# One core, attention over kept tokens: the first pair's products in four PSUM banks, other buffers and slots for the first two batches

## The chip, the cores and the metric

The kernel runs on one core of a Trainium2 chip. The metric is device time in microseconds. The engines that compute are TensorE (PE, with PEld for its weight loads), VectorE (DVE), ScalarE (ACT) and GpSimd (POOL); SyncE (SP) issues DMAs. Each has its own instruction stream and runs it in order; they wait for each other by semaphores.

## What is computed

Eight batches of attention with eight heads, with queries, keys and values from one projection, a 0/1 mask over tokens, and a residual. From the reference:

```python
B, D, T = x.shape                 # 8, 512, 1024
dk = D // NH                      # 8 heads of 64
xt = jnp.transpose(x, (0, 2, 1))
q = xt @ Wq.T
qh = q.reshape(B, T, NH, dk).transpose(0, 2, 1, 3)
scores = scale * jnp.einsum('bhqd,bhkd->bhqk', qh, qh)
logits = (scores * cmask + (1.0 - cmask) * NEG) * rmask
attn = jax.nn.softmax(logits, axis=-1)
ctx = jnp.einsum('bhqk,bhkd->bhqd', attn, qh)
out = ctx.transpose(0, 2, 1, 3).reshape(B, T, D) @ Wo.T
return x + jnp.transpose(out, (0, 2, 1))
```

A masked token (mask 0) as a key gets weight 0; as a query it attends evenly to all tokens, so that its output is the mean of all values.

## The kernel before

About half of the 1,024 tokens of a batch are kept by the mask. The kernel gathers the kept tokens, at most 543 (`NK` = `SHORT` = 544 places, the last one for the mean of all tokens), and runs attention on them alone. Inputs with more kept tokens go to two other versions, which don't run here.

**Pairs and slots.** The work is 32 pairs: 8 batches of 4 pairs of heads (`pairs`, numbered p; `pr` is the pair in its batch). A pair has five slots, k = 0 to 4, one for each chunk of 128 keys, in `order`: first the short chunk `LAST` (with tokens 512 to 575 of the ring), then the four full ones. In each slot `late` issues `scores` of that chunk (TensorE, line 785 or 807; exponentials by ScalarE, line 793 or 810), and then what the tables give to slot (pr, k): `TURN`, `SEARCH`, `GATHER`, `LOAD`, `FEATURES` and others. For the second batch the tables with `_LATER` hold, and `LATER` for its search. Last come the tasks of `slots_of`, among them `attend_half` (line 831), `project` (703) and `collect` (659). The order on each engine is the order in the program: `manual_schedule` moves nothing.

**A batch's way in.** `load_piece` loads x in eight pieces of 256 KB, two halves of the tokens (tag `x`, two buffers). `turn` transposes a quarter of the tokens on VectorE (581) into a buffer `xt` (two of them), whose four stores to DRAM (`xd`) SP issues at the end of the slot (589). `search` finds on VectorE (634, 637), for each place, which token it holds, from the ranks that `load_ranks` has broadcast. `gather` fetches the rows of the kept tokens from `xd` by an indirect DMA on POOL (646), five of them, the fifth with 32 rows; `keep_step` ahead of it makes POOL wait for an exponential of that slot. `collect` turns the rows back on TensorE (659) and a copy puts them into `xcs`; `project` multiplies them by Wq. For the second batch the collects are in slots (2,3) and (2,4). `add_features` sums x over tokens on ScalarE (600), `mean_of` makes the mean on VectorE (605, 607).

**The ring.** `rings[0]` holds the projection of the first pair: 544 columns, and from column `NK` on the last 32 columns (`END`) three times over.

**The first batch and `early`.** The first pair of the first batch takes another way, so as not to wait for a gather. `early` counts the kept tokens, makes ranks and `chosen` (0/1 matrices that select tokens, `choose`, 444), and calls `project_first`. There TensorE turns a part of Wq (482), `search_first` broadcasts the ranks by sixteen matmuls (451) and ScalarE counts by `Sign` with a sum (464), five times; `project_all` multiplies blocks of 128 tokens, all of them, by that part of Wq (493), from block 7 down to 0, into `tall`, one PSUM tile of two banks. `copy_two` (503) copies two blocks to `q`, `square` (510) squares four for `lengths` (513). `order_columns` (1171) reorders Wq on ScalarE. On VectorE come two `turn_first` (423), `choose`, `sources_of_first` (475, which needs the signs), the other two `turn_first`, pads and penalties (534 to 537), and the lengths up to `first_top` (546). The products `short` (555) select the kept tokens' columns from `q`; among them stands the transpose of `first_top` (764) that gives the first bias (766 to 769). `add_first` (435) sums x on VectorE. ScalarE copies `short` to the ring (568).

Then `late` begins, behind a branch that each engine takes by itself when it gets there. VectorE copies the ring's end columns there (1322), POOL issues the first batch's gathers (646), the load of the second batch's ranks (622) and of Wo (1162), and SP loads the second batch's x (385), whose buffers come free when `add_first` has read the first batch's.

Of the kernel before, what the change touches and what calls it, by code (L numbers as in the profile page):

```python
# [10 lines left out]
F32 = mybir.dt.float32  # L11
# [10 lines left out]
Q = 32  # L22
# [284 lines left out]
def attention_of_kept_tokens(ctx, tc, x, mask, wq, wo, out, ident, wqT, woT, verdict, flag):  # L307


    nc = tc.nc  # L310
# [107 lines left out]
    def turn_first(i):  # L418

        n = T // NQ  # L420
        r, at = divmod(i * n, NB)
        xt = sb.tile([P, n // Q, P], F32, tag="xt", name=f"xt_0_{i}", bufs=2)
        nc.vector.transpose(
            xt.rearrange("p k (d f) -> p k d f", d=ND),
            xs[0][r][:, :, at : at + n].rearrange("p d (k t) -> p k d t", t=Q),
        )
        for a in range(A):
            to = xds[0][i * n : (i + 1) * n, a * P : (a + 1) * P]
            queue = nc.gpsimd if a % 2 else nc.sync
            queue.dma_start(to.rearrange("(k t) c -> t k c", t=Q), xt[a * Q : (a + 1) * Q, :, :])  # L430

    def add_first(r):
        if r == NN - 1:
            xbars[0] = keep.tile([P, ND, NN], F32, name="xbar_0")
        nc.vector.tensor_reduce(xbars[0][:, :, r], xs[0][r], axis=AX.X, op=ALU.add)
# [41 lines left out]
    def project_first(chosen, mcol):  # L477

        wT = sb.tile([P, ND, P], F32, tag="junka", name="wqT_0", bufs=1)
        pw = bank("wq_0_t")  # L480
        for d in range(ND):
            nc.tensor.transpose(pw[:, d * P : (d + 1) * P], woT[:, 0, d::ND], ident)
        nc.scalar.copy(wT.rearrange("p d e -> p (d e)"), pw)
        search_first(seen["rank"])
        tall = ps.tile([P, 2, NB], F32, tag="s", name="tall")
        q = [sb.tile([P, G, P], F32, tag="oc", name=f"q_0_{r}", bufs=NC) for r in range(NN)]
        sq = sb.tile([P, T], F32, tag="junk", name="sq_0", bufs=1)
        H = LONG // 2

        def project_all(i):  # L490
            r, at = divmod(i * P, NB)
            for d in range(ND):
                nc.tensor.matmul(
                    tall[:, r, at : at + P],
                    xs[0][r][:, d, at : at + P],
                    wT[:, d, :],
                    start=(d == 0),
                    stop=(d == ND - 1),
                )

        def copy_two(i):
            r, at = divmod(i * P, NB)
            nc.scalar.copy(
                q[r][:, i % G : i % G + 2, :].rearrange("p c e -> p (c e)"),
                tall[:, r, at : at + 2 * P],
            )

        def square(r):
            at = slice(r * NB, (r + 1) * NB)
            nc.scalar.activation(sq[:, at], tall[:, r, :], AF.Square)  # L510

        def lengths(r):
            nc.vector.tensor_reduce(
                first_len[:, r * G : (r + 1) * G, :].rearrange("p c h -> p (c h)"),
                sq[:, r * NB : (r + 1) * NB].rearrange("p (c d) -> p c d", d=DK),
                axis=AX.X,
                op=ALU.add,
            )

        for i in reversed(range(NT)):  # L520
            project_all(i)
            if i % 2 == 0:
                copy_two(i)
            if i % G == 0:
                square(i // G)
        order_columns()
        turn_first(2)
        turn_first(3)
        for i in (3, 2, 1, 0):
            choose(i, chosen[i])  # L530
# [6 lines left out]
        nc.vector.tensor_scalar(pens, pads, NEG, None, ALU.mult)  # L537
        lengths(1)
        lengths(0)
        nc.vector.tensor_tensor(  # L540
            first_len,
            first_len,
            mcol[:, :NT].unsqueeze(2).to_broadcast([P, NT, 2]),
            ALU.mult,
        )
        nc.vector.tensor_reduce(
            first_top, first_len.rearrange("p c h -> p (c h)"), axis=AX.X, op=ALU.max
        )
        short = ps.tile([P, 2, NB], F32, tag="s", name="short")
        for i in reversed(range(NT)):  # L550
            w = chosen[i].shape[1]
            for hf in range(2):
                n = min(w - hf * H, H)
                if n > 0:
                    nc.tensor.matmul(
                        short[:, hf, :n],
                        q[i // G][:, i % G, :],
                        chosen[i][:, hf * H : hf * H + n],
                        start=(i == NT - 1),
                        stop=(i * P <= hf * H),  # L560
                    )
            if i == G:
                tops[pairs[0]] = first_top
                bias_of(pairs[0], first_bias)
        add_first(1)
        add_first(0)
        mean_of(0)
        nc.scalar.copy(
            rings[0][:, :LONG].rearrange("p (h n) -> p h n", h=2), short[:, :, :H]
        )  # L570

    def turn(b, i):
# [609 lines left out]
            )  # L1182
        (copy or nc.scalar.copy)(wT[:, d, :], pt)

    def early():
        BC = B * NT
        mrow = keep.tile([BC, P], F32, name="mrow")
        nc.sync.dma_start(mrow, mask.rearrange("b (c p) -> (b c) p", p=P))
# [118 lines left out]
        nc.vector.tensor_copy(origin, placed)  # L1307

    def late(n):
        fit_to(n)  # L1310
        nc.vector.tensor_scalar(lacks, kept, float(-NK), None, ALU.add)
        queries_of(0)
        load_batch(1)
# [2 lines left out]
        for i in range(NC):  # L1316
            gather(0, i)
        load_ranks(1, nc.gpsimd)
        weights["wo"] = load_weights(wo, "wo", nc.gpsimd)
        qT = qTs[pairs[0]] = rings[0]  # L1320
        biases[pairs[0]] = first_bias
        nc.vector.tensor_copy(
            qT[:, NK:W].rearrange("p (r k) -> p r k", k=END),
            qT[:, NK - END : NK].unsqueeze(1).to_broadcast([P, (W - NK) // END, END]),
        )
# [176 lines left out]
def kernel(  # L1502
# [22 lines left out]
    def kept_tokens(n):  # L1525

        with ExitStack() as pools:
# [1 line left out]
                pools, tc, x, mask, wq, wo, out, ident, wqT, woT, verdict, flag  # L1529
            )  # L1530
            with tc.manual_schedule():
                early()
# [41 lines left out]
```

## Time and profile before

| | us |
|---|---|
| Median of three runs | 702.32 (700.89 to 702.73) |
| The profiled execution | 700.78 |
| Its span, first to last instruction | 699.0 |
| PE busy in the span | 657.0 (94%) |
| PEld busy | 400.1 (57%) |
| DVE busy | 366.5 (52%) |
| ACT busy | 395.0 (57%) |
| POOL busy | 181.6 (26%) |
| mean granted TensorE clock | 0.968 |

Busy is the time in which an engine had an instruction under way. The chain of waits starts at the last instruction and goes back, at each step, to what released it; its shares say where time was spent that something else would have had to take. In the timeline a line gives start and length in us, engine, source line and operation, output and inputs by the program's names, how many instructions were merged, and in brackets the idle time before the first and what ended it. A window gives, for a stretch of the span, each engine's busy time, and the clock that TensorE was granted as a share of full speed.

### The profile page before, as it was taken

The page shows a single profiled execution, that of the slowest core. Times are in us where ns is not written, and L with a number is a line of the kernel's source. Part 1 is how long each engine was busy: PE and PEld are TensorE (multiplying, and loading weights), DVE is VectorE, ACT ScalarE, POOL GpSimd, SP SyncE. Part 2 cuts the span into 40 slices and gives each one's busy share as a digit, 9 for nine tenths or more (in the row PEclk, how much of TensorE's full clock was granted, in tenths as well). Part 3 has the DMA queues.
Part 4 walks back from the last instruction along what each step waited for, and adds up shares of the span by engine and source line. Part 5 has one row for each costly group of instructions (what it writes and reads, how often), then busy time and mean ns, then how long its engine had stood idle before and what let it go on. Part 6 is the DMA issues. An engine that isn't in the chain of part 4 may idle for free.

```text
span 699.0 us, 12228 instructions
## 1 busy us (share of the span) xinstructions
PE 657.0 (94%) x4212; PEld 400.1 (57%) x4212; DVE 366.5 (52%) x1061; ACT 395.0 (57%) x1055; POOL 181.6 (26%) x304
## 2 busy tenths in 40 slices
PE   8799979999999999999999999999999999999953
PEld 7666546656565655556565655556565655554422
DVE  5555864435556554756446653837455433724462
ACT  4347747855576556746585656755574655444400
POOL 4700310040034402440044302450143202332240
PEclk7999989999999999999999999999999999999975
DMA  7552560442856577765786477864974575348558
GB/s 244 161 206 81 162 182 2 119 160 88 185 157 214 163 176 164 216 211 138 181 216 230 157 174 167 257 225 110 205 185 126 124 159 125 107 115 215 121 185 242
DMA packets 99169, 116.31 MB, mean 166 GB/s; under 512 B 10471, under 2 KB 76519, under 8 KB 99102
## 3 DMA queue, kind: packets, MB, share of 16 engines
q1 hardware_dynamic: 82894, 77.23, 42.9%
q0 software_dynamic: 11984, 36.16, 16.3%
q10 hardware_dynamic: 4224, 2.10, 1.0%
q8 instruction: 34, 0.56, 0.3%
q14 instruction: 33, 0.27, 0.1%
HBM read 72.78 MB, written 42.67 MB: 165 GB/s over the span
## 4 chain that ended last, share of the span: by engine, by line
PE 77%; DMA 9%; DVE 4%; issue 2%; ACT 1%; SPq 1%; POOL 0%; POOLq 0%; DVEq 0%; ACTq 0%
PE s L785 19%; PE av L831 17%; PE po L952 14%; PE pq L703 14%; DMA g<-od,block_origin 3%; PE xc L659 3%; PE s L807 3%; PE v L728 2%; PE pa L980 2%; DMA xr<-in_x_dram 1%; PE top L764 1%; DVE xr L1029 1%; DMA xin<-xd,source 1%; DMA xd<-xt 1%; DMA g<-od,origin 1%
## 5 line engine op out<-in xcount | busy, mean ns | idle before, releaser
L793 ACT ACTIVATE e<-s,bias 128x544 f32<-128x544 f32 x248 | 174.7, 709 | 68.0 <-PE s L785 65.8
L785 PE MATMUL s<-qT 64*128 64x272 f32 x1024 | 168.4, 418 | 1.0 <-issue 0.7
L785 PEld LDWEIGHTS s<-qT 64*128 64x128 f32 x1024 | 97.5, 187 | 67.8 <-issue 29.7
L831 PE MATMUL av<-e,v 128*64 128x272 f32 x1024 | 133.1, 403 | 0.0
L703 PE MATMUL pq<-xc,wqT 128*128 128x272 f32 x496 | 119.3, 393 | 0.0
L952 PE MATMUL po<-woT,cT 128*128 128x512 f32 (+1 forms) x448 | 107.5, 434 | 0.0
L703 PEld LDWEIGHTS pq<-xc,wqT 128*128 128x128 f32 x496 | 93.1, 193 | 17.8 <-issue 0.8
L831 PEld LDWEIGHTS av<-e,v 128*64 128x64 f32 x1024 | 68.5, 138 | 56.7 <-issue 24.4
L964 POOL DMA_DIRECT2D od<-oc x56 | 30.2, 551 | 254.9 <-ACT oc L962 254.7
L952 PEld LDWEIGHTS po<-woT,cT 128*128 128x128 f32 (+1 forms) x448 | 46.8, 150 | 47.0 <-issue 46.2
L1066 POOL DMA_INDIRECT g<-od,block_origin x56 | 56.4, 1007 | 50.2 <-DVE o L1026 12.4
L1026 DVE STREAM_TRANSPOSE o<-g 128x512 f32<-128x512 f32 x56 | 39.3, 702 | 35.9 <-DMA g<-od,block_origin 34.4
L822 DVE CUSTOM_DVE_ANT_0 junk<-el,part 128x272 f32<-128x272 f32 x64 | 28.1, 438 | 54.9 <-ACT el L810 43.8
L810 ACT ACTIVATE el<-s,bias 128x544 f32<-128x544 f32 x31 | 22.1, 714 | 57.5 <-PE s L807 56.4
L1062 POOL COPY step<-e 1x1 f32<-1x1 f32 x77 | 16.7, 217 | 142.0 <-ACT e L793 141.6
L711 ACT COPY qT<-pq 128x272 f32<-128x272 f32 (+1 forms) x62 | 23.6, 381 | 51.7 <-PE pq L703 49.1
L751 DVE TENSOR_REDUCE len<-sq 128x10 f32<-128x640 f32 x31 | 25.3, 817 | 47.4 <-ACT sq L749 47.4
L793 ACT ACTIVATION_READ_ACCUMULATOR e<-s,bias 128x1 f32 x248 | 48.6, 196 | 0.0
L1029 DVE TENSOR_TENSOR xr<-o,xr 128x512 f32<-128x512 f32 x56 | 38.8, 693 | 14.5 <-DMA xr<-in_x_dram 8.0
L646 POOL DMA_INDIRECT xin<-xd,source x40 | 39.7, 993 | 16.8 <-issue 8.8
L766 DVE TENSOR_REDUCE m<-top 128x1 f32<-128x128 f32 x32 | 9.2, 289 | 57.8 <-PE top L764 55.8
L581 DVE STREAM_TRANSPOSE xt<-x 128x1024 f32<-128x1024 f32 x28 | 34.8, 1242 | 3.2 <-DMA xd<-xt 3.1
(183 smaller groups left out, 718.3 us busy)
## 6 DMA issues: line engine op xcount, KB each, us to landing
x<-in_x_dram SPq DMA_DIRECT2D x64, 256.0 KB
xd<-xt SPq DMA_DIRECT2D x120, 128.0 KB
xr<-in_x_dram SPq DMA_DIRECT2D x28, 512.0 KB
out_dram<-xr SPq DMA_DIRECT2D x24, 512.0 KB
rb<-row SPq DMA_DIRECT2D x60, 160.0 KB
od<-oc POOLq DMA_DIRECT2D x28, 256.0 KB
rank<-ranks SPq DMA_DIRECT2D x6, 512.0 KB
out_dram<-xr SPq DMA_DIRECT2D x8, 256.0 KB
```

Source lines behind the costliest of these rows:

```text
L581: nc.vector.transpose(xt.rearrange("p k (d f) -> p k d f", d=ND), xs[b][r][:, :, at : at + n].rearrange("p d (k t) -> p k d t", t=Q),)
L646: nc.gpsimd.indirect_dma_start(out=xin[:n, :], out_offset=None, in_=xds[b], in_offset=bass.IndirectOffsetOnAxis(ap=searches[b][2][:n, i : ...
L703: nc.tensor.matmul(pq[:, :KH], wqT[:, d, pr * P : (pr + 1) * P], xcs[b][:, d, cols], start=(d == 0), stop=(d == ND - 1),)
L785: nc.tensor.matmul(ss[h][:, hf, :KH], qT[heads[h], keys], qT[heads[h], queries[hf]], start=True, stop=True,)
L793: nc.scalar.activation(e[:, :, h, :], ss[h][:, :, :KH], AF.Exp, bias=bias, scale=SCALE, accum_out=sums[pair[1] % 2][:, h, c : c + 1],)
L822: nc.vector.tensor_tensor_reduce(junk[:, :KH], e[:, 0, h, :], parts[b], 1.0, 0.0, ALU.mult, ALU.add, ends[pr % 2][:, h : h + 1])
L831: nc.tensor.matmul(av[head, :KH], v[keys, c, head], e[keys, hf if c < LAST else 0, h, :], start=(c == first), stop=(c == last),)
L952: nc.tensor.matmul(po[k * n : (k + 1) * n, :w], cTs[b, pr][:, i * P : i * P + n], woT[:, pr, k * w : (k + 1) * w], start=(pr == 0), stop=( ...
L964: nc.gpsimd.dma_start(ods[b][places[i], k * w : (k + 1) * w], oc[k * n : (k + 1) * n, :w])
L1026: nc.vector.transpose(o.rearrange("p k t -> p (k t)"), gs[b, i])
L1029: nc.vector.tensor_tensor(to, o, to, ALU.add)
L1066: nc.gpsimd.indirect_dma_start(out=g, out_offset=None, in_=ods[b], in_offset=bass.IndirectOffsetOnAxis(ap=block_origin[:, b, i : i + 1], a ...
```

## The change

The first batch's products go to four PSUM banks of one tile each, two blocks to a bank. `search_first` moves from ahead of all products to behind the first four blocks (7 to 4), their copies and `square(1)`, with eight transposes of the identity (`warm(8)`) in its old place. The squares read `q` in SBUF; `square(0)` comes after the last copy. `turn_first` takes its buffers from the tag `e` (six buffers, used later by the exponentials), so four quarters have one each; for that `fit_to` is called in `early`. `add_first` and `mean_of` go ahead of the lengths. The transpose of `first_top` goes from behind block 4 to behind block 2 of `short`. The ring's end columns are copied from `short` by ScalarE. In the tables, the second batch's turns, searches and gathers move.

```diff
@@ turn_first
-        xt = sb.tile([P, n // Q, P], F32, tag="xt", name=f"xt_0_{i}", bufs=2)
+        xt = sb.tile([P, 2, 2, KH], F32, tag="e", name=f"xt_0_{i}", bufs=6)
+        xt = xt.rearrange("p a b k -> p (a b k)")[:, : n // Q * P].rearrange("p (k c) -> p k c", c=P)
@@ project_first
-        search_first(seen["rank"])
-        tall = ps.tile([P, 2, NB], F32, tag="s", name="tall")
+        warm(8)
+        tall = [bank(f"tall_{i}") for i in range(NT // 2)]
...
-        sq = sb.tile([P, T], F32, tag="junk", name="sq_0", bufs=1)
+        sq = {}
...
-                    tall[:, r, at : at + P],
+                    tall[i // 2][:, i % 2 * P : (i % 2 + 1) * P],
...
-                q[r][:, i % G : i % G + 2, :].rearrange("p c e -> p (c e)"),
-                tall[:, r, at : at + 2 * P],
+                q[i // G][:, i % G : i % G + 2, :].rearrange("p c e -> p (c e)"),
+                tall[i // 2][:, : 2 * P],
...
         def square(r):
-            at = slice(r * NB, (r + 1) * NB)
-            nc.scalar.activation(sq[:, at], tall[:, r, :], AF.Square)
+            t = sb.tile([P, NC, P], F32, tag="sq", name="sq_0_1", bufs=1) if r else sb.tile(
+                [P, NT, P], F32, tag="junk", name="sq_0_0", bufs=1
+            )
+            sq[r] = t[:, :G, :].rearrange("p c e -> p (c e)")
+            nc.scalar.activation(sq[r], q[r].rearrange("p c e -> p (c e)"), AF.Square)
...
             project_all(i)
             if i % 2 == 0:
                 copy_two(i)
-            if i % G == 0:
-                square(i // G)
+            if i == G:
+                square(1)
+                search_first(seen["rank"])
+        square(0)
         order_columns()
...
         nc.vector.tensor_scalar(pens, pads, NEG, None, ALU.mult)
+        add_first(1)
+        add_first(0)
+        mean_of(0)
         lengths(1)
         lengths(0)
...
-            if i == G:
+            if i == 2:
                 tops[pairs[0]] = first_top
                 bias_of(pairs[0], first_bias)
-        add_first(1)
-        add_first(0)
-        mean_of(0)
         nc.scalar.copy(
             rings[0][:, :LONG].rearrange("p (h n) -> p h n", h=2), short[:, :, :H]
         )
+        nc.scalar.copy(
+            rings[0][:, NK:W].rearrange("p (r k) -> p r k", k=END),
+            short[:, 1, NK - END - H : NK - H].unsqueeze(1).to_broadcast([P, (W - NK) // END, END]),
+        )
@@ early, late
-    def early():
+    def early(n):
+        fit_to(n)
...
-        fit_to(n)
...
-        qT = qTs[pairs[0]] = rings[0]
+        qTs[pairs[0]] = rings[0]
         biases[pairs[0]] = first_bias
-        nc.vector.tensor_copy(
-            qT[:, NK:W].rearrange("p (r k) -> p r k", k=END),
-            qT[:, NK - END : NK].unsqueeze(1).to_broadcast([P, (W - NK) // END, END]),
-        )
...
-        TURN_LATER = [(0, 4), (1, 0), (1, 1), (1, 2)]
+        TURN_LATER = [(0, 3), (0, 4), (1, 0), (1, 1)]
...
-        LATER = {(1, 1): (0,), (1, 2): (1,), (1, 3): (2, 3), (1, 4): (4,)}
+        LATER = {(0, 4): (0,), (1, 0): (1,), (1, 1): (2,), (1, 2): (3,), (1, 3): (4,)}
...
-        GATHER_LATER = {(1, 4): (0,), (2, 0): (1,), (2, 1): (2,), (2, 2): (3,), (2, 3): (4,)}
+        GATHER_LATER = {(1, 4): (0, 1), (2, 0): (2,), (2, 1): (3,), (2, 2): (4,)}
```

More of the change, by code (lines that the diff above doesn't have):

```diff
@@ L501, in copy_two @@
         def copy_two(i):
-            r, at = divmod(i * P, NB)
             nc.scalar.copy(
-                q[r][:, i % G : i % G + 2, :].rearrange("p c e -> p (c e)"),
-                tall[:, r, at : at + 2 * P],
+                q[i // G][:, i % G : i % G + 2, :].rearrange("p c e -> p (c e)"),
+                tall[i // 2][:, : 2 * P],
             )
         def square(r):
-            at = slice(r * NB, (r + 1) * NB)
-            nc.scalar.activation(sq[:, at], tall[:, r, :], AF.Square)
+            t = sb.tile([P, NC, P], F32, tag="sq", name="sq_0_1", bufs=1) if r else sb.tile(
[3 more added lines that the diff above has]
+            nc.scalar.activation(sq[r], q[r].rearrange("p c e -> p (c e)"), AF.Square)
         def lengths(r):
@@ L514, in lengths @@
                 first_len[:, r * G : (r + 1) * G, :].rearrange("p c h -> p (c h)"),
-                sq[:, r * NB : (r + 1) * NB].rearrange("p (c d) -> p c d", d=DK),
+                sq[r].rearrange("p (c d) -> p c d", d=DK),
                 axis=AX.X,
@@ L1531, in kept_tokens @@
             with tc.manual_schedule():
-                early()
+                early(n)
             fit = nc.values_load(verdict[0:1, 0:1], min_val=0, max_val=2 * T)
```

## The prediction

> **What bounds the kernel now.** I read the page first, for which engine the chain of waits runs on; then the chain itself over the first 130 us, since the diff touches only the first batch's start and the slots of the second batch; then the timeline around the two places where the chain leaves TensorE; last the windows, cut where the granted clock changes.
>
> ```profile
> PE 77%; DMA 9%; DVE 4%; issue 2%; ACT 1%; SPq 1%; POOL 0%; POOLq 0%; DVEq 0%; ACTq 0%
> ```
>
> TensorE carries 77% of the chain, so a microsecond taken from a place where it waits should go through to the end. The chain in order of time (start, length, what):
>
> ```profile
> 35.64 0.91 PE s L807 x8
> ...
> 57.43 0.62 PE s L807 x8
> ...
> 58.75 0.62 PE av L831 x8
> 59.36 1.12 PE s L785 x8
> ...
> 86.24 0.27 issue
> 86.51 6.84 DMA xin<-xd,source
> ...
> 94.09 1.11 PE s L807 x8
> 95.20 0.91 PE av L831 x8
> 96.11 1.78 PE s L785 x8
> ```
>
> A gather of the second batch holds the chain for 6.84 us, and the three steps after it are slower than the same three at 57 us. In the first 40 us the timeline shows (start, length, engine, line, op, tiles, count, idle time before):
>
> ```profile
> 7.61 2.84 PE L451 MATMUL ranks<-rank_row,ident 64*128 64x128 f32 x16
> ...
> 10.38 3.78 PE L493 MATMUL tall<-wqT,x 128*128 128x128 f32 x16
> 10.55 1.11 ACT L464 ACTIVATE sign<-ranks,half 128x1024 f32<-128x1024 f32 x1 [2.25 <-PE ranks L451]
> ...
> 15.45 0.19 ACT L464 ACTIVATION_READ_ACCUMULATOR sign<-ranks,half 128x1 f32 x1
> ...
> 15.75 0.17 DVE L475 SCALAR_TENSOR_TENSOR source<-found,middle 128x5 int32<-128x5 f32 x1 [2.47 <-ACT sign L464]
> 15.95 3.45 PE L493 MATMUL tall<-wqT,x 128*128 128x128 f32 x16 [1.79 <-ACT q L503]
> ...
> 20.02 0.18 DVE L537 TENSOR_SCALAR pens<-pads 128x40 f32<-128x40 f32 x1
> ...
> 20.36 2.05 PE L493 MATMUL tall<-wqT,x 128*128 128x128 f32 x16 [0.96 <-ACT sq L510]
> ...
> 24.77 4.05 PE L555 MATMUL short<-chosen,q 128*128 128x288 f32 x16
> ...
> 25.87 0.69 DVE L513 TENSOR_REDUCE first_len<-sq 128x8 f32<-128x512 f32 x1 [4.84 <-ACT sq L510]
> ...
> 26.80 0.17 DVE L546 TENSOR_REDUCE first_top<-first_len 128x1 f32<-128x16 f32 x1
> ...
> 29.61 4.47 DVE L435 TENSOR_REDUCE xbar<-x 128x4 f32<-128x2048 f32 x2
> 30.04 0.87 POOL L646 DMA_INDIRECT xin<-xd,source  x1 [0.30 <-issue]
> ...
> 31.18 0.64 ACT L568 COPY qT<-short 128x576 f32<-128x576 f32 x1 [1.29 <-PE short L555]
> ...
> 35.26 0.24 DVE L1322 COPY qT<-qT 128x96 f32<-128x96 f32 x1
> 35.64 0.91 PE L807 MATMUL s<-qT 64*64 64x272 f32 x8 [4.50 <-DVE qT L1322]
> ```
>
> TensorE stands still for 1.79 us behind ScalarE's signs, then for 0.96 us, then for 4.50 us: the ring of the first pair is copied at 31.82, but its end columns come from VectorE, which is busy with the sums of features until 34.08. What the clock does with such gaps (stretch, its length, busy PE, PEld, DVE, ACT, POOL, granted clock, DMA share, GB/s):
>
> ```profile
> 0.00:8.40 8.40, 6.98 (x37) 5.62 (x38) 3.25 (x15) 2.34 (x4) 5.10 (x21) 1.00 0.68 208
> ...
> 15.49:18.91 3.42, 2.96 (x14) 2.96 (x15) 2.86 (x6) 0.41 (x3) 1.22 (x3) 0.50 0.30 94
> ...
> 32.56:35.98 3.42, 0.34 (x8) 0.24 (x8) 2.29 (x8) 0.00 (x0) 3.06 (x5) 1.00 0.96 252
> 35.98:39.39 3.41, 3.41 (x20) 2.41 (x14) 1.59 (x3) 0.81 (x2) 0.00 (x0) 0.50 0.97 354
> ...
> 90.59:97.41 6.82, 3.92 (x26) 2.44 (x28) 4.44 (x22) 1.07 (x3) 0.36 (x1) 0.50 0.42 129
> ```
>
> After the 4.50 us gap the clock is 0.50 for one stretch of 3.41 us, after the gather's wait for two. A stretch with 2.96 us of products brought it back to full.
>
> **Part one, the start.** In the diff the rank products and the signs go behind the first four blocks of products, their two copies and square(1); eight warm-up transposes take their old place. The products get four banks, so TensorE waits for no copy. The first products need the second half of x: by 8.40 us 208 GB/s have moved 1.75 MB, and that half with what is queued ahead of it is 1.34 MB, so I start them at 8.5 rather than 10.38. At half clock sixteen product matmuls take 3.78 us, at full clock 2.05. The stretch of 3.41 us before 12.08 is then all products and should end at full clock: about 16 of the 32 by 12.08, the other 16 in 2.05 us, 14.1. The sixteen rank matmuls took 2.84 us, mostly at half clock, and 2.84 × 2.05/3.78 = 1.5 would be full clock throughout; I take 1.9, so 16.0. The copy of 256 columns and the square of 512 are done by then (576 columns take ScalarE 0.64). The signs run from 10.55 to 15.64 now, 5.09 us, and the sources are ready 0.28 later, at 15.92. **After the change the sources come at 16.0 + 0.1 + 5.09 + 0.28 = 21.5 us, 5.6 later than before.** VectorE is in order, so its whole tail is queued behind this wait: two transposes, the keys and pads up to 20.20 (4.28 us after the sources, less 0.23 that it waited for a buffer of turned x, which four buffers remove: 4.05), now the two sums and the mean (4.47 and two small operations like the 0.17 ones, 4.9 with their starts), then the lengths (two reductions of 0.69 and two of 0.17 and 0.18, 1.8). The greatest length is thus ready at 21.5 + 4.05 + 4.9 + 1.8 = 32.2; before, at 26.97.
>
> TensorE meanwhile ends the products of tokens 0 to 511 near 20 and the ring's first 24 matmuls (4.05/16 = 0.25 each or less) near 25.3, and then stands at the transpose of that greatest length, which now comes ahead of the last four. It waits some 7 us, where it waited 4.50 later. The clock will have dropped, so transpose and last four take about 1.7: 33.9. ScalarE copies the ring (0.64) and its end columns (0.24, by VectorE's copy of the same size), with hand-overs 35.1. **First scores at 35.1 instead of 35.64: −0.55 us.** The 4.50 us gap isn't removed; it is moved ahead of the ring's last products, and the copy, sums and stall only change places.
>
> Bounds. If the clock stays at half until 15.49, the sources come 1.4 later and the first scores at 36.5: +0.85. If the stretch from 32.56 counts as busy (some 2.4 of 3.41 us; 2.96 did), full clock returns at 35.98 instead of 39.39 and another 1.4 is saved: −1.95. I take −0.55, the value with the clock's rows as they stand.
>
> One rule speaks against this part. The Trainium skill, "TensorE: Matmul & The Clock Gate", section "Part 1: The HAM clock gate", says that one idle window of about 3.4 us puts the clock back to half. The trace agrees (0.50 after the 4.50 us gap); by it the 7 us gap costs half clock on the last ring products, which the 1.7 above has; without it that step would be some 0.7 shorter and the time 695.6.
>
> The first batch's gathers read what the late transposes store, so they start 5.6 later: the last, at 30.04 now, at 35.6. Their cover is the slack until TensorE turns their rows.
>
> **Part two, the second batch's slots.** The rows (same columns):
>
> ```profile
> 42.92 1.09 PE L659 MATMUL xc<-ident,xin 128*128 128x128 f32 x8
> ...
> 45.77 1.48 DVE L663 COPY xc<-xc 128x512 f32<-128x512 f32 x3 [0.86 <-PE xc L659]
> ...
> 47.17 1.23 DVE L581 STREAM_TRANSPOSE xt<-x 128x1024 f32<-128x1024 f32 x1
> ...
> 54.54 0.82 DVE L751 TENSOR_REDUCE len<-sq 128x10 f32<-128x640 f32 x1 [6.14 <-ACT sq L749]
> ...
> 83.39 0.96 POOL L646 DMA_INDIRECT xin<-xd,source  x1 [0.57 <-DVE source L637]
> 83.46 4.38 SPq L385 DMA_DIRECT2D x<-in_x_dram  x8
> ...
> 89.13 0.63 PE L659 MATMUL xc<-ident,xin 128*128 128x128 f32 x4 [1.00 <-DVE cT L936]
> ...
> 93.49 0.60 PE L659 MATMUL xc<-ident,xin 32*128 32x32 f32 x4 [3.73 <-DMA xin<-xd,source]
> ```
>
> The turns move one slot or more ahead, the searches likewise, and the fifth gather goes from slot (2,3) to (2,2): from 86.51 to where the fourth goes now, 83.39. The other four go out a slot earlier too, or with the one before. A turn in slot (0,3) puts 1.23 us on VectorE ahead of three copies that the next projection waits for; 0.86 of idle time takes most of it: **+0.4**. The turn and search in (0,4) fall into the 6.14 us that VectorE idles before 54.54. Slot (1,0) gets a search beside its turn (a scan of 1,024 numbers, like the turn some 1.2); what of it TensorE sees at the next top I put at nothing, because (1,1) to (1,3) lose a turn; uncovered it would cost 1. The stores of turned x go out on SP a slot earlier; no row transfer is passed. The fourth gather took from 83.39 to about 89.1, 5.7 us, among the eight loads of x that SP issues from 83.46 on; the fifth, with 32 rows, will do so now. TensorE could turn its rows at 89.13 − 1.00 + 0.63 = 88.8, so it waits 0.3 instead of 1.00 + 3.73: **−4.4**. Without the idle time the clock stays up: the three steps cost 1.11 + 0.91 + 1.78 = 3.80 now, 0.62 + 0.62 + 1.12 = 2.36 at full clock: **−1.44**. Bound: if the fifth gather takes its 6.84 us again, it lands at 90.3 and 1.5 is waited, 1.2 worse.
>
> **Sum.** −0.55 + 0.4 − 4.4 − 1.44 = −6.0. The profiled execution took 700.78 (span 699.0), so 694.8 for one like it; the median of the runs shown, 702.32, lies 1.5 above it, so **696.3**.
>
> The Trainium skill, "DMA: Bandwidth & Descriptors", section "Queues, rings and completion order", says that each DMA engine takes turns between queues packet by packet. By that the small fifth gather would not wait behind SP's loads at all, and the 0.3 would go: 696.0; the 6.84 us row speaks against it.
>
> **The rivals.** (1) The fifth gather keeps its 6.84 us and the wait of 1.5 brings a half-clock stretch with it: 696.3 + 1.2 + 1.44 = 698.9. For it: the 6.84 and 5.7 us rows. Against: 64 KB, and an issue ahead of seven of the eight loads. (2) The moved slots don't do what they say: the fifth gather lands only as the eight loads are through, near 93.4, whenever it is issued. Then only the 1.00 before it goes, with −0.55 and +0.4: 702.32 − 1.15 = 701.2. For it: it landed about when the loads ended. Against: the fourth landed in their middle. (3) The clock is not back by 12.08: 697.7. (4) Slower: the late search. Every microsecond by which the sources come after 21.5 goes through VectorE's tail to the first scores. From 27.5 on it has eaten the second batch's 6.0, and at 30 the time is 704.8. It would take the rank products and signs to run behind all eight blocks of products (about 27.2, 702.0) and one more late transfer. For it: nothing covers this chain, and TensorE already waits on its end. Against: on both engines the signs are ahead of the last four blocks. A late gather of the first batch adds nothing before that: even at 6.84 the last lands by 35.6 + 6.84 = 42.4, the first two some 4 us sooner, and TensorE turns the first two blocks at 42.92, the last three just ahead of the copies at 45.77, both less 0.55.
>
> **How the numbers follow.** Forecast 0.58, (1) 0.15, (2) 0.12, (3) 0.07, (4) 0.08. A measurement of this kernel tells 0.3%, 2.1 us, from no change. Faster: forecast, (1), (3), 0.80; same: (2), 0.12; slower 0.08. The range leaves (2) and (4) out. Low end: 694.8, less 1.4 for the clock back at 35.98, 0.4 and 0.3 not paid, 692.7 (from the profiled execution, the shorter one). High end: rival (1) with the late clock of (3), 698.9 + 1.4 = 700.3.
>
> **What would show it.** Source at 21 to 22 us; a TensorE gap of some 7 us that ends at the top of the first pair near 32; first L807 near 35; the fifth gather issued near 83, no wait of several microseconds at L659 after it, and a granted clock of 1.00 from 87 to 97. Wrong would be: first scores before 33 or after 37, or the 6.84 us step still in the chain.

## The result, and the profile after

| | before | changed |
|---|---|---|
| Median, 20 runs each | 701.23 us (697.52 to 702.89) | 696.5 us (690.77 to 708.55) |
| Ratio, 95% interval | | 0.9928 (0.9908 to 0.9949) |
| Profiled execution, its span | 700.78, 699.0 us | 697.53, 695.8 us |
| Mean granted clock | 0.968 | 0.974 |

Forecast was 696.3, and 6.0 us less than before; measured are 4.7 by the two medians. Two profiles of one kernel differ by more than that (below: the kernel before has spans of 699.0 and 691.6), so single profiles are read here for where things happen, and times for how much. Ratios leave out runs more than 1.5% above the fastest of their kernel, medians don't, so the two can differ.

The page of the changed kernel gives (busy time, share of the span, instructions):

```profile
PE 657.8 (95%) x4220; PEld 401.7 (58%) x4220; DVE 367.7 (53%) x1060; ACT 394.7 (57%) x1056; POOL 181.2 (26%) x304
```

No engine's busy time falls by more than 0.4 us, and TensorE's grows by 0.8; the 3.2 us between the spans come from less waiting. The timeline of the changed kernel's start (columns as in the prediction; "first scores" below is the start of its last line, "sources" the end of the line at L476):

```profile
9.02 1.91 PE L441 MATMUL warm<-ident 128*128 128x128 f32 x8
10.72 5.22 PE L494 MATMUL tall<-wqT,x 128*128 128x128 f32 x32
15.87 2.05 PE L452 MATMUL ranks<-rank_row,ident 64*128 64x128 f32 x16
17.85 3.84 PE L494 MATMUL tall<-wqT,x 128*128 128x128 f32 x32
18.02 1.11 ACT L465 ACTIVATE sign<-ranks,half 128x1024 f32<-128x1024 f32 x1 [1.01 <-PE ranks L452]
21.52 5.59 PE L563 MATMUL short<-chosen,q 128*128 128x288 f32 x24
...
23.22 0.17 DVE L476 SCALAR_TENSOR_TENSOR source<-found,middle 128x5 int32<-128x5 f32 x1 [8.77 <-ACT sign L465]
27.39 4.47 DVE L436 TENSOR_REDUCE xbar<-x 128x4 f32<-128x2048 f32 x2
32.19 1.27 DVE L516 TENSOR_REDUCE first_len<-sq 128x8 f32<-128x512 f32 x2
34.02 0.45 PE L773 MATMUL top<-ident,first_top 128*128 128x128 f32 x1 [6.91 <-DVE first_top L554]
35.78 0.64 ACT L573 COPY qT<-short 128x576 f32<-128x576 f32 x1 [7.42 <-issue]
36.74 1.19 PE L816 MATMUL s<-qT 64*64 64x272 f32 x8 [1.00 <-ACT qT L573]
```

The products run without a gap, as they should with four banks; the first 32 take 5.22 us and the other 32, at full clock, 3.84, so the clock came up in the middle of the first. But the sources come at 23.39 instead of 15.92, VectorE stands 8.77 us for them, and its tail (sums, lengths, top) then holds TensorE for 6.91 us: the 4.50 us gap ahead of the first scores has become one of 6.91 ahead of the top, and 1.00 behind it. The first scores start at 36.74, where the profile before had 35.64.

Around the end of the second batch's gathers, the timeline of the changed kernel:

```profile
81.31 4.86 SPq L385 DMA_DIRECT2D x<-in_x_dram  x8
...
83.56 0.90 POOL L655 DMA_INDIRECT xin<-xd,source  x1 [0.59 <-DVE mean L616]
...
89.95 0.40 PE L668 MATMUL xc<-ident,xin 32*128 32x32 f32 x4 [1.76 <-DMA xin<-xd,source]
90.28 0.69 PE L816 MATMUL s<-qT 64*64 64x272 f32 x8
```

Waits of 1.00 and 3.73 us have become one of 1.76, and the scores behind it run at full clock, as a window of the changed kernel says (columns as in the prediction):

```profile
30.90:34.35 3.45, 0.33 (x2) 0.36 (x3) 2.83 (x7) 0.00 (x0) 2.23 (x3) 0.50 0.89 289
87.00:97.00 10.00, 8.24 (x64) 5.24 (x62) 9.22 (x37) 5.42 (x14) 1.93 (x2) 1.00 0.45 155
```

The first line lies almost wholly in the 6.91 us gap and shows the half clock that it brings; the last four ring products run at it.

To cut the time into stretches I use the first exponential of each pair, whose scores run first in that pair. ScalarE's rows, first of the kernel before, then of the changed one:

```profile
36.60 0.71 ACT L810 ACTIVATE el<-s,first_bias 128x544 f32<-128x544 f32 x1 [4.78 <-PE s L807]
58.31 0.71 ACT L810 ACTIVATE el<-s,bias 128x544 f32<-128x544 f32 x1 [0.30 <-DVE bias L769]
73.76 0.70 ACT L810 ACTIVATE el<-s,bias 128x544 f32<-128x544 f32 x1
95.27 0.71 ACT L810 ACTIVATE el<-s,bias 128x544 f32<-128x544 f32 x1 [0.88 <-PE s L807]
```

```profile
38.00 0.71 ACT L819 ACTIVATE el<-s,first_bias 128x544 f32<-128x544 f32 x1 [1.31 <-issue]
60.05 0.71 ACT L819 ACTIVATE el<-s,bias 128x544 f32<-128x544 f32 x1 [0.31 <-DVE bias L778]
75.50 0.70 ACT L819 ACTIVATE el<-s,bias 128x544 f32<-128x544 f32 x1
91.03 0.71 ACT L819 ACTIVATE el<-s,bias 128x544 f32<-128x544 f32 x1 [0.39 <-PE s L816]
```

Start +1.40; first pair to second 21.71 against 22.05, +0.34; second to third 15.45 both times; third to fourth, where the second batch is collected, 21.51 against 15.53, −5.98. Sum −4.24 at the fourth pair.

Not all of the −5.98 lies at the gathers. Early in the third pair the kernel before has a wait that the trace puts down to a copy of `v`, and behind it sixteen products at half clock (0.50 from 76.93 to 80.35); the changed kernel has neither. First before, then changed:

```profile
75.09 0.68 PE L831 MATMUL av<-el,v 64*64 64x272 f32 x4 [1.34 <-ACT v L736]
...
76.81 3.74 PE L831 MATMUL av<-e,v 128*64 128x272 f32 x16
```

```profile
77.36 2.06 PE L840 MATMUL av<-e,v 128*64 128x272 f32 x16
```

The waits of the stretch shrink from 1.34 + 1.00 + 3.73 = 6.07 to 1.76, 4.31 less, and these sixteen products are 1.68 shorter: together 5.99, so that what else changes there about cancels.

The spans differ by only 3.2. Part of what lies between the −4.24 and this is a late residual load in the last batch, which the changed kernel's profile shows:

```profile
648.55 0.69 DVE L1038 TENSOR_TENSOR xr<-o,xr 128x512 f32<-128x512 f32 x1 [10.49 <-DMA xr<-in_x_dram]
...
655.74 2.40 PE L888 MATMUL rb<-ident,ris 128*64 128x128 f32 x20 [2.08 <-DVE ris L909]
```

VectorE, in order, adds five residual pieces (648.55 to 654.63) before it makes `ris`, and TensorE waits 2.08 us for that. From the last pair's first exponential to the end this execution takes 64.4 us, the profile before 60.0. A second profile of the changed kernel takes 60.0, so this is of the execution, not of the change.

### The profile page after: what moved, and what is told of

It is laid out like the page before. It is cut to its first block, busy times and chain, and to the rows that moved or that the text cites. A ratio compares the mean times of both kernels' runs of the same rounds, so it can differ in the third digit from the quotient of the medians.

```text
span 695.8 us, 12245 instructions
## 1 busy us (share of the span) xinstructions
PE 657.8 (95%) x4220; PEld 401.7 (58%) x4220; DVE 367.7 (53%) x1060; ACT 394.7 (57%) x1056; POOL 181.2 (26%) x304
## 5 line engine op out<-in xcount | busy, mean ns | idle before, releaser
L609 ACT ACTIVATE junka<-x 128x512 f32<-128x512 f32 x56 | 35.1, 627 | 0.4
```

What stands on the lines that cost most here:

```text
L609: nc.scalar.activation(junk, xs[b][r][:, d, :], AF.Copy, accum_out=xbars[b][:, d, r : r + 1])
```

## Experiments

Ratios are to the kernel before on the same chip, with 95% intervals.

**The start alone, and the slots alone.** From the changed kernel, the three `_LATER` tables as before (twice); from the kernel before, only these three tables changed (twice).

```diff
-        TURN_LATER = [(0, 3), (0, 4), (1, 0), (1, 1)]
+        TURN_LATER = [(0, 4), (1, 0), (1, 1), (1, 2)]
...
-        LATER = {(0, 4): (0,), (1, 0): (1,), (1, 1): (2,), (1, 2): (3,), (1, 3): (4,)}
+        LATER = {(1, 1): (0,), (1, 2): (1,), (1, 3): (2, 3), (1, 4): (4,)}
...
-        GATHER_LATER = {(1, 4): (0, 1), (2, 0): (2,), (2, 1): (3,), (2, 2): (4,)}
+        GATHER_LATER = {(1, 4): (0,), (2, 0): (1,), (2, 1): (2,), (2, 2): (3,), (2, 3): (4,)}
```

> The changed kernel with the second batch's three tables as before. Theory (the whole gain lies in the slots, the start gives nothing or loses up to 1.5 us): the ratio to the kernel before is 0.999 to 1.003, some 701 to 703 us; first scores at 36 to 37 us, and TensorE waits 3 us or more for the fifth gather again. Rival (the start brings part of the gain): ratio 0.998 or less, below 700 us.

> The kernel before with the second batch's three tables as changed, and nothing else. Theory: all of the gain, ratio 0.991 to 0.993, some 695 to 696.5 us; first scores at 35.6 as before, the wait for the fifth gather under 1.8 us and the clock at full from 87 to 97 us. Rival (the slots need the earlier loads that the new start gives): the turns wait for x, the wait at the fifth gather stays over 3 us, ratio above 0.997.

> The kernel of e1_front_only again. What is open: like for like in the clock's start the profiles give the new start 2.5 to 3.6 us, but its timed runs gave nothing. Theory (the start gains): ratio 0.995 to 0.997. Rival (what it gains is given back where the fifth gather waits): ratio 1.000, and first exponentials no later than 38.2 us, but the stretch from the third pair's first exponential to the fourth's 2 us or more longer than in the changed kernel (15.5 to 16.0 us).

> The kernel of e2_slots_only again. Theory (the slots' part is some 2.4 us, the mean of the waits seen so far): ratio 0.9955 to 0.9975, the stretch from the third pair's first exponential to the fourth's 15.5 to 16.5 us. Rival (the slots carry the whole gain, as forecast): ratio 0.992 to 0.994.

Start alone: 700.3 us, 0.9998 (0.997 to 1.0026), and 700.08, 0.996 (0.9929 to 0.9991). Slots alone: 698.15, 0.9977 (0.9951 to 1.0004), and 696.74, 0.9954 (0.9926 to 0.9982). By the ratios the slots alone give 1.6 and 3.2 us and the whole change 5.0. The first theory, that all of the gain is in the slots, is unlikely by that: the interval of the first run of the slots alone lies outside that of the whole change, that of the second reaches into it. What the start gives by itself stays between nothing and some 3 us: the ratio of 0.996 has its interval below 1, but the medians behind it (700.08 against 699.32 for the kernel before on that chip) show no gain.

In their profiles the start alone waits 1.58 us for the fifth gather, not the 3 or more expected, and the second time 1.42 and 2.42 for the last two; third pair to fourth takes 16.53 and 20.60 us. The slots alone wait 2.15 and 2.21 us, with 15.95 and 15.99 from third pair to fourth, so they do what was expected of them there, and still bring less time than expected. First scores come at 36.93 and 36.34 with the new start and at 40.37 and 37.95 with the old one.

Why the two profiles of before and after showed the start as a loss is seen in the first profile of the slots alone, whose start is word for word the old one:

```profile
12.86 3.78 PE L493 MATMUL tall<-wqT,x 128*128 128x128 f32 x16
...
23.19 3.78 PE L493 MATMUL tall<-wqT,x 128*128 128x128 f32 x16 [0.96 <-ACT sq L510]
...
29.49 4.05 PE L555 MATMUL short<-chosen,q 128*128 128x288 f32 x16
...
40.37 1.18 PE L807 MATMUL s<-qT 64*64 64x272 f32 x8 [4.50 <-DVE qT L1322]
```

Sixteen product matmuls take 3.78 us as late as 23.19; the kernel before had 2.05 at 20.36. TensorE's clock came up later in this execution, and the same instructions reach the first scores at 40.37 instead of 35.64. (The windows' clock column reads 1.00 from 12.86 to 16.64 and from 23.19 to 26.97 here all the same. In the kernel before, 3.78 us for sixteen of these matmuls stood beside a clock of 0.50, so in the first microseconds I go by their lengths.) From the first ring product on, the old start is the same every time: 24.77 to 35.64 is 10.87 us, 29.49 to 40.37 is 10.88. So what differs is when in an execution the clock goes to full, called its phase here; it decides where the ring products start, and one pair of profiles can't price a start. The Trainium skill, "TensorE: Matmul & The Clock Gate", section "Part 1: The HAM clock gate", has the activity window run free of the kernel, so that the moment of full clock differs from run to run. The trace agrees in kind; the section's ±500 ns, given for sustained matmuls, is far less than the 4.7 us seen here, where they come in bursts.

**The end columns alone.** The kernel before, with the one copy moved to ScalarE and `fit_to` in `early` for it, nothing else.

```diff
+        nc.scalar.copy(
+            rings[0][:, NK:W].rearrange("p (r k) -> p r k", k=END),
+            short[:, 1, NK - END - H : NK - H].unsqueeze(1).to_broadcast([P, (W - NK) // END, END]),
+        )
...
-        qT = qTs[pairs[0]] = rings[0]
+        qTs[pairs[0]] = rings[0]
...
-        nc.vector.tensor_copy(
-            qT[:, NK:W].rearrange("p (r k) -> p r k", k=END),
-            qT[:, NK - END : NK].unsqueeze(1).to_broadcast([P, (W - NK) // END, END]),
-        )
```

> The kernel before with one edit: the ring's end columns by ScalarE from PSUM, for which the sizes are set in early. Theory (the 4.50 us gap was the wait for VectorE's end of sums): with the clock full from about 5 us first scores at 32.2 instead of 35.6, of which VectorE's copies of Wq's transposes give back about 1: ratio 0.996 to 0.9975. Rival (the gap comes from something else, or is waited for later): first scores early, ratio 1.000.

Measured: 694.64 us, 0.993 (0.9902 to 0.9958), better than the theory, whose 0.996 lies just outside the interval. The timeline of this kernel:

```profile
27.29 4.05 PE L555 MATMUL short<-chosen,q 128*128 128x288 f32 x16
...
32.14 4.47 DVE L435 TENSOR_REDUCE xbar<-x 128x4 f32<-128x2048 f32 x2
...
34.38 0.24 ACT L571 COPY qT<-short 128x96 f32<-128x96 f32 x1
34.67 0.69 PE L811 MATMUL s<-qT 64*64 64x272 f32 x8 [1.00 <-ACT qT L571]
```

From the first ring product to the first scores it is 34.67 − 27.29 = 7.38 us instead of 10.87: 3.49 less, and the scores run while the sums of features are still on VectorE. The wait of 4.50 has shrunk to the 1.00 of the copy's hand-over. The interval of the ratio, −2.9 to −6.9 us, holds this 3.5.

**What the late search and the early sums cost.** From the changed kernel, once the search back ahead of all products (in the place of the warm-up transposes), once the sums and the mean back behind the bias.

```diff
-        warm(8)
+        search_first(seen["rank"])
...
                 square(1)
-                search_first(seen["rank"])
```

> The changed kernel with the ranks' matmuls and signs back ahead of all products, in place of the eight warm-up transposes. Theory (the late search holds VectorE's whole tail and so the first scores): sources near 16 us, the gap of 7 us before the first pair's top is under 3 us, first scores at 31 to 33 us, and the kernel is 3 to 5 us faster than the changed one, 691.5 to 693.5. Rival (the gap is set by sums and lengths, not by the search): sources early but first scores still at 35 or later, time as the changed kernel's.

```diff
         nc.vector.tensor_scalar(pens, pads, NEG, None, ALU.mult)
-        add_first(1)
-        add_first(0)
-        mean_of(0)
         lengths(1)
...
                 bias_of(pairs[0], first_bias)
+        add_first(1)
+        add_first(0)
+        mean_of(0)
```

> The changed kernel with the two sums of features and the mean back behind the first bias. Theory: the greatest length comes 4.9 us sooner, first scores 4 to 5 us sooner (near 32), but VectorE's copies of Wq's transposes then wait for the sums until about 35.5, so of this 1 to 3 us is left: 693.5 to 695.5. Rival (the sums sooner were worth their place): TensorE stalls as long behind those copies as it gained, time as the changed kernel's or longer.

690.08 us, 0.9863 (0.9826 to 0.99), and 690.61, 0.9877 (0.984 to 0.9914): both faster than the kernel before by more than the changed kernel (0.9928, 0.9908 to 0.9949) and than was expected. The first interval lies outside the changed kernel's, the second overlaps it a little; each has six runs. Search first:

```profile
18.23 0.17 DVE L476 SCALAR_TENSOR_TENSOR source<-found,middle 128x5 int32<-128x5 f32 x1 [3.78 <-ACT sign L465]
...
29.03 0.29 PE L772 MATMUL top<-ident,first_top 128*128 128x128 f32 x1 [1.63 <-DVE first_top L553]
30.98 0.69 PE L815 MATMUL s<-qT 64*64 64x272 f32 x8 [1.00 <-ACT qT L575]
```

Sums late:

```profile
25.45 0.29 PE L773 MATMUL top<-ident,first_top 128*128 128x128 f32 x1 [2.10 <-DVE first_top L551]
26.44 4.47 DVE L436 TENSOR_REDUCE xbar<-x 128x4 f32<-128x2048 f32 x2
27.95 1.19 PE L816 MATMUL s<-qT 64*64 64x272 f32 x8 [1.00 <-ACT qT L576]
```

The gap of 6.91 us is cut to 1.63 and 2.10. Counted from the first ring product, so that the clock's phase before it drops out, the first scores come 15.22 us later in the changed kernel (36.74 − 21.52), 9.16 with the search first (30.98 less its 21.82) and 10.19 with the sums late (27.95 less its 17.76): 6.1 and 5.0 us less. The cause has two halves, late sources and sums ahead of the lengths; taking away either one removes most of the gap. In the second the sums lie beside the scores, where the changed kernel had them ahead of the top.

**Both kernels again.**

> The kernel before, unchanged, profiled again. Theory (the start depends on when the clock first goes to full, the wait for the fifth gather on whether SP's loads of x are issued ahead of it): ratio 1.000; where the clock is full from about 5 us, first scores at 35.6, where only later, at 38 to 40.5; the fifth gather takes 5.5 to 7 us if four or more loads are issued ahead of it and some 4 us if not. Rival (the first profile is what every execution does): first scores at 35.6, wait of 4.7 us.

> The changed kernel, unchanged, profiled again. Theory: ratio 0.992 to 0.994; with the clock full from about 5 us the sources come near 19.6 and the first scores at 32.5 to 33.5, with a later clock at 23.4 and 36.7; wait for the fifth gather 1 to 2 us. Rival: first scores at 36.7 whatever the clock.

The kernel before: 698.05 us, 1.0023 (0.9998 to 1.0049), span 691.6. The changed one: 693.61, 0.9942 (0.9909 to 0.9975), span 690.4. The changed kernel waits 2.24 us for the fifth gather this time (1.76 in its first profile) and takes 16.01 us from the third pair's exponential to the fourth's (15.53 then). But the kernel before takes only 17.14, not 21.51. Its timeline there:

```profile
84.23 4.08 SPq L385 DMA_DIRECT2D x<-in_x_dram  x8
...
84.92 0.90 POOL L646 DMA_INDIRECT xin<-xd,source  x1 [0.58 <-PE xc L659]
...
89.92 0.40 PE L659 MATMUL xc<-ident,xin 32*128 32x32 f32 x4 [2.92 <-DMA xin<-xd,source]
```

Its gather went out 0.69 us behind the first load of x; in the first profile 3.05 behind (86.51 after 83.46). TensorE had the rows 5.00 us after the issue here and 6.98 there. The half clock in front of the gathers is missing too: the wait of 1.34 us for `v` stands here as well, but the sixteen products behind it take 2.06 us, not 3.74. What the change removes there is thus not a constant of the kernel before.

The wait of 1.34 us is in all profiles with the old turns and searches (the kernel before and the start alone, twice each, and the end columns alone) and in none with the new ones, also not with the gathers back in their old slots (below). So the turns and searches remove it; the half clock follows it in two of the five.

**When the gathers go out.** From the changed kernel, the gathers' table as before; and the last two gathers a slot sooner still.

```diff
-        GATHER_LATER = {(1, 4): (0, 1), (2, 0): (2,), (2, 1): (3,), (2, 2): (4,)}
+        GATHER_LATER = {(1, 4): (0, 1), (2, 0): (2, 3), (2, 1): (4,)}
```

> The changed kernel with the table of the second batch's gathers as before (the fifth in slot (2,3)), its turns and searches as changed. Theory (the fifth gather's place against the loads of x is what counts): the loads are issued ahead of it, it takes 6 to 7 us, TensorE waits 4 to 5 us and the kernel is 3 to 5 us slower than the changed one, ratio 0.997 to 1.000. Rival (the earlier turns and searches do it): the wait stays under 2 us and the time is the changed kernel's.

> The changed kernel with the fourth gather in slot (2,0) and the fifth in (2,1), one slot sooner. Theory: the fifth is issued about 80 us, ahead of the loads of x at 81, lands before 85, and TensorE waits for none of the gathers: 1.5 to 2.5 us off the changed kernel, ratio 0.989 to 0.991. Rival (the wait has moved to something else, or the search isn't ready): no difference from the changed kernel.

As before: 695.5 us, 0.9967 (0.9935 to 0.9999). Sooner: 689.63, 0.9887 (0.9848 to 0.9926). On this chip the changed kernel has 0.9942 (0.9909 to 0.9975); both intervals overlap its own, so the times alone tell neither from it for sure, and the 3 to 5 us expected of the old table are 1.9 by the medians. With the old table in the changed kernel the fourth and fifth rows wait again:

```profile
91.17 0.63 PE L668 MATMUL xc<-ident,xin 128*128 128x128 f32 x4 [3.34 <-DMA xin<-xd,source]
...
92.17 0.43 PE L668 MATMUL xc<-ident,xin 32*128 32x32 f32 x4 [0.37 <-DMA xin<-xd,source]
```

With the gathers sooner:

```profile
77.42 0.90 POOL L655 DMA_INDIRECT xin<-xd,source  x1 [0.16 <-PE s L794]
78.12 4.23 SPq L385 DMA_DIRECT2D x<-in_x_dram  x8
...
83.56 1.45 PE L668 MATMUL xc<-ident,xin 128*128 128x128 f32 x12
```

The fifth gather is issued 0.70 us ahead of the loads and nothing waits for it: third pair to fourth 14.20 us, 1.8 less than in the changed kernel on this chip. Two things changed at once, though. TensorE comes for the fifth rows at 84.58, 7.16 us after the issue, so that gathers of 5.00 and 6.98 us, as in the kernel before, would have been in time too. And in the first profile of the start alone it was issued 0.11 us ahead of the loads, and TensorE waited 1.58 us for it. Being ahead of the loads is thus not enough by itself, and the slot sooner may do without it; no run separates the two.

This profile also shows what an early clock makes of the new start, in which no instruction differs (its first 32 products take 3.80 us, not 5.22):

```profile
19.26 0.17 DVE L476 SCALAR_TENSOR_TENSOR source<-found,middle 128x5 int32<-128x5 f32 x1 [6.19 <-ACT sign L465]
...
30.05 0.45 PE L773 MATMUL top<-ident,first_top 128*128 128x128 f32 x1 [6.91 <-DVE first_top L554]
...
32.78 1.18 PE L816 MATMUL s<-qT 64*64 64x272 f32 x8 [1.00 <-ACT qT L576]
```

Sources at 19.43 and first scores at 32.78, 3.96 before the changed kernel's own profile; the gap is 6.91 again.

**All three improvements together** (search first, sums late, gathers sooner).

> The changed kernel with three edits together: the search ahead of all products (as e3_search_first), the sums behind the first bias (as e4_sums_late), the fifth gather in slot (2,1) (as e7_gather_sooner). Theory (they take different waits: ScalarE's copies set the first scores near 28 us, and no gather is waited for): faster than each of them, ratio 0.979 to 0.983, 685 to 688 us on a chip where the kernel before takes 700. Rival (the same gap counted three times): ratio 0.985 or more.

689.71 us, 0.9874 (0.9853 to 0.9895): no better than each alone, as the rival had it. What the theory said of the waits held (first scores at 27.23, no wait for a gather), but that is hardly sooner than with the sums late alone, and then TensorE waits for what had time before:

```profile
36.54 1.12 PE L667 MATMUL xc<-ident,xin 128*128 128x128 f32 x4 [2.24 <-DVE wqT L1191]
```

```profile
35.70:45.80 10.10, 9.26 (x32) 6.79 (x33) 7.87 (x13) 1.50 (x4) 0.52 (x1) 0.50 0.86 289
```

First in the timeline, VectorE's copy of another part of Wq, now late, holds the first collect for 2.24 us; then in the windows ten microseconds at half clock. First to second pair takes 27.78 us (27.98 to 55.76) where the changed kernel takes 22.05. The four versions with the search first, the sums late, the gathers sooner and all three have medians below both kernels (0.9863 to 0.9887 of the kernel before); none is told from the others.

## Why the prediction held, step by step

**The late search and the gap.** Right in mechanism: VectorE's whole tail is queued behind the sources, and TensorE stands at the top of the first pair for "some 7 us"; 6.91 in both clock phases. The sources were put at 21.5; they came at 23.39 in the profile, where the clock was late, and at 19.43 where it was early (first scores then at 32.78, outside the 33 to 37 that was given as a sign). Rival (3), clock not back by 12.08, with first scores at 36.5, is what the changed kernel's profile shows (36.74). That the last ring products run at half clock after the gap held too: 1.49 us for four, 0.82 with the search first.

**The step "first scores: −0.55 us"** seems mis-sized. It was worked out against the 35.64 of one execution with an early clock. The old start in five profiles (the kernel before twice, slots alone twice, ends alone) begins its ring products at 24.77, 24.88, 29.49, 27.09 and 27.29, on average 26.70; with the constant 10.87 this is first scores at 37.6. The new start in five (the changed kernel twice, the start alone, both gather tables) has 36.74, 36.20, 36.93, 36.84 and 32.78, on average 35.9. That is −1.7, inside the bounds of +0.85 and −1.95, and inside the nothing to 3 us that the times leave. But each five spread over more than 4 us, and the phases aren't mixed alike. Where ScalarE's first copy of Wq's transposes (L483 or L484) starts between 7.5 and 7.9 us, the old start has 35.64, 35.73 and 37.95, the new 32.78; where it starts near 9.26, the old has 40.37 and, with the constant, 38.16, the new 36.74, 36.20, 36.93 and 36.84. Like for like that is some 2.6 to 3.7 less, so −1.7 is the least that the profiles suggest, and few profiles stand behind either. With −3.5 for the end columns, as the kernel with these alone shows, all else in the start about cancels: like for like the ring products begin some 7 to 8 us sooner in the new order (17.56 to 21.71 against 24.77 to 29.49), and from there to the first scores it takes 15.22 us instead of the 7.38 with the end columns alone, 7.84 more, by the late search and the early sums. "The 4.50 us gap isn't removed; it is moved" was true of the whole change, but it hid that one edit does remove it and the search and sums put another in its place.

**The turn in slot (0,3): +0.4.** Measured +0.34 between the first two profiles (21.71 to 22.05, from first pair to second).

**The gathers: −4.4 and −1.44, together −5.84.** Between the first two profiles −5.98, nearly the forecast, but made up of other things. The wait at the gathers fell by 2.97, not 4.4: the fifth one's was put at 0.3 and is 1.76, near the 1.5 of the bound and of rival (1). The rest is the wait of 1.34 for `v` and the half clock at 76.81, two rows that the prediction did not read; the half clock that it did price lies at the stretch's end and mostly behind it. That the sum agreed is luck. The first profile was also a long one.

Over four profiles with the old tables (the kernel before 21.51 and 17.14, start alone 16.53, ends alone 20.15; mean 18.8) and four with the new ones (the changed kernel 15.53 and 16.01, slots alone 15.95 and 15.99; mean 15.9) the term is −2.9; with the second profile of the start alone, of a long execution of 702.25 us, it is −3.3 (20.60; mean 19.2). What the working left out is that SP's loads of x went out sooner too, 81.31 instead of 83.46, and so still ahead of the fifth gather. Rival (2), that the gather lands only with the last load, is out: 1.76 us of wait is left, not 3.73. Rival (1) had the wait about right, but the half clock that it expects behind it does not follow.

**The sum.** −1.7 + 0.3 − 2.9 = −4.3 against −4.7 by the medians and −6.0 in the forecast. That the time came out at 696.5 beside 696.3 is in part luck: the mis-sized terms pulled in opposite directions (the start some 1.1 better, the gathers 2.9 worse), and the kernel before measured 701.23 over 20 runs, 1.1 below the median from which the forecast started, which made up for most of the 1.3 by which the difference fell short.

**The slower rival**, a late search that eats the gain, was right in its mechanism and wrong in its point: the search did cost microseconds, but the sources came 4 us before the 27.5 from which it would have decided.

**Open.** How often each clock phase occurs; how large the start's gain is by time (0.9998 and 0.996); what holds back a gather's first packet beside the loads (last section); whether the end columns alone and the new slots would add up, which was not run; why the last batch's residual load is late in some executions.

## What to carry over

When one copy holds the path because its engine is busy with something else, try that copy alone on an idle engine before rearranging the rest: here it gave about as much (0.993, 0.9902 to 0.9958) as the whole change (0.9928, 0.9908 to 0.9949). A wait that varies between executions must be priced over several profiles, since the longest one shown is likely the one that invites the change. Gains found one at a time needn't add up, since what they uncover behind them takes its share: 0.9863, 0.9877 and 0.9887 alone, 0.9874 together.

## What the hardware showed beside this

The clock's phase at the start is worth up to 4.7 us with the same instructions (first scores at 35.64 and 40.37), as much as the whole change gains.

Half clock followed the wait of 1.34 us in two of the five profiles that have it (sixteen products in 3.74 us in the kernel before, in 3.73 in the second of the start alone) and did not in the other three (2.05 or 2.06). So a wait that short can be followed by half clock, and need not be; what decides it is not shown.

A gather of 64 KB that was issued behind the first of eight 256-KB loads reached TensorE 5.00, 6.39 and 6.98 us after its issue (the kernel before again, the changed one, the first profile). The DMA packets in these traces say where the time goes. The gather's first packet ran 2.71, 4.08 and 4.14 us after its issue, and TensorE had the rows 2.3 to 2.8 us after that. The first gather of the second batch, with no such load under way, had its first packet 1.79 us after its issue in the first profile. Beside the loads the gather thus starts to move data 0.9 to 2.4 us later: 0.9 where it was issued 0.69 us behind the first of them, 2.3 and 2.4 where it was 2.25 and 3.05 behind. That it is not the distance alone is seen in the end columns alone, where it was 1.06 behind, had its first packet after 4.73 us and reached TensorE after 7.30. One issued 0.11 and one 0.70 us ahead of them had their first packets after 2.32 and 2.36 us (the start alone, the gathers sooner).

The Trainium skill, "DMA: Bandwidth & Descriptors", section "Queues, rings and completion order", has each DMA engine take turns between its queues packet by packet; if that spared a small transfer, the 1.76 us would not be there. The trace does not agree with that reading. It puts the delay ahead of the gather's first packet, and does not show whether its packets were in the queue by then.
